# Attention and mixture of experts: the scatters of token assignments, one tile at a time

## The chip, the cores and the metric

The kernel runs on one NeuronCore of one Trainium2 chip. The metric is the device time of one execution in microseconds. Before the change it is 1081.88 us, the median of three runs (1081.15 to 1082.97).

A core has five engines, each with an instruction queue of its own that is worked off in order: TensorE (PE in the profile; its weight loads are PEld), VectorE (DVE), ScalarE (ACT), GpSimd (POOL) and SyncE (SP). Transfers are issued by SyncE, by ScalarE or, where rows are gathered or scattered by an index, by GpSimd.

## The reference

4096 tokens of 256 float32 values pass a causal attention and then a mixture of 8 experts, each with a layer norm ahead and the input added behind:

```python
x = x + attn(layernorm(x), Qw, Kw, Vw)      # softmax(Q K^T / sqrt(256) + causal mask) V
x = x + ffn(layernorm(x), ...)

def ffn(x):
    t = x @ W_in + b_in
    probs = softmax(t @ W_gate + b_gate)    # 8 experts
    topv, topi = top_k(probs, 2)            # each token goes to 2 experts
    topv = topv / sum(topv)
    for e in range(8):
        eout[e] = relu(t @ W1[e] + b1[e]) @ W2[e] + b2[e]      # 256 -> 1024 -> 256
    return sum_over_its_2_experts(topv * eout) @ W_out + b_out
```

So 8192 assignments of a token to an expert have to be sorted by expert, since the kernel computes only the two experts of each token.

## The kernel before

**Tiling.** A token block is 512 tokens (`TB`), that is 4 tiles of 128 (`TPB`), and there are 8 blocks (`NB`). A query tile is 256 tokens (`QB`), so there are 16 of them, numbered `g`, two to a block.

**Attention.** The loop at L1079 runs over `g`. Each turn records `scores(g + 1)` and then `attend(g)`. `scores` goes over chunks `c` of 256 keys up to the diagonal: 8 matmul records into one PSUM bank `ps` (tag `mm`, four buffers, L555), a copy to SBUF on ACT (`s`, L564), and from the second chunk on a running maximum on DVE (`mx`, L570). Between the `mx` of the first chunks stands `fill`: pieces of layer norm and transposes for later blocks, which `keep_in_program_order` pins one behind the other. `finish` (L594) transposes the maximum, subtracts it (DVE, L612) and exponentiates (ACT, L615). `attend` multiplies with the values (`po`, L633).

**Routing.** A block behind, `enter` (L353) makes `t` and the gate's logits of a block, writes `t` to the DRAM tensor `rows`, and `route` (L386) picks the two experts of each token, counts how many tokens each expert has had, and so finds each assignment's slot (`at`, L440). `slots` is a DRAM table with a stretch for each expert. `route` casts the four slot numbers of each of its two choices (`k`) to integers (`ati`, L441) and then issues, for each choice and tile, an indirect DMA from GpSimd that scatters 128 assignment numbers, 16 integers (`LINE`) each, to their slots (L443). That is 8 scatters to a block, 64 in all. They are declared free of dependence on one another, since slots are distinct.

The scatters of blocks 0 to 5 follow the attention of query tiles 3, 5, 6, 8, 10 and 12. Block 6 is routed in the middle of query tile 14 (`find`, L1112). Block 7, the last, is routed in the experts' loop at work item 1 (L1260).

**Other work on GpSimd.** Its queue also has the two steps of 1/sqrt(variance) of each layer norm (`ln_rstd`, L261 and L262), the addition of the output's bias to the residual (`x<-x,bout`, L1250), the gathers of expert rows (`h`, L824) and the scatters of results (`parts`, L997).

**Experts.** `plan` (L653) cuts each expert's slots into units. The work list has 17 units of kind a and 8 of kind b (256 slots, one expert), 8 of c (128 slots), 6 of d (twice 64 slots of two experts, two more only where needed) and one of z (256 late slots). Kind a is planned before query tile 14 from blocks 0 to 5, and its units read only slots of these. The loop at L1228 keeps three units ahead (`AHEAD`): `fetch_rows` loads a unit's slots (SyncE, L808) and gathers its rows (L824); `fetch_weights` loads four tiles of 512 KB for each expert and small biases (SyncE, L861 to L878) into buffers that an earlier unit frees; `turn_rows` transposes the rows on DVE (`hT`, L901); `hidden` does the first layer (`pm`, L921, activation on ACT at L930); `contribute` does the second (`pe`, L988), adds the bias on DVE (`y`, L996) and scatters (L997). At work item 3 the kernel takes the late unit: `take_late` (L752) loads 256 slots (`late_slot`, L762) and overwrites them in the table (`none`, L763). It has to wait for all scatters to `slots`, and what stands behind it in SyncE's queue, unit 7's slots and unit 6's weights first, waits with it. Here is the chain of these items in the code:

```python
take_late()                                        # L1231, at n == AHEAD
got[n + AHEAD + 1] = fetch_rows(work[n + AHEAD + 1])     # L1240
got[weighed] += fetch_weights(work[weighed], ...)        # L1243
```

**Order.** Within an engine the recording layer may move instructions that depend on nothing between them, but not those that `keep_in_program_order` pins. Tiles with a tag share its `bufs` buffers in turn, and the next user of a buffer waits for the last reader of the one before.

Of the kernel before, what the change touches and what calls it, by code (L numbers as in the profile page):

```python
# [37 lines left out]
def preln_attention_moe_kernel(  # L38
# [314 lines left out]
    def enter(b, zT, pool, behind=False):  # L353
# [29 lines left out]

        return lg

    def route(b, lg, seen, pool, behind=False):  # L386


        def small(name, w=1):
            return pool.tile([P, TPB, w], F32, tag=name, name=f"{name}{b}", bufs=2)  # L390

        def wide(a):
            return a.to_broadcast([P, TPB, NE])


        top = [small(f"top{k}") for k in range(TOPK)]
        hot = [small(f"hot{k}", NE) for k in range(TOPK)]
        prob, best = small("prob", NE), small("best")
        nc.vector.tensor_reduce(best, lg, AX.X, ALU.max)
        nc.vector.tensor_tensor(lg, lg, wide(best), ALU.subtract)  # L400
        nc.scalar.activation(prob, lg, AF.Exp)
        left = prob
        for k in range(TOPK):
            nc.vector.tensor_reduce(top[k], left, AX.X, ALU.max)
            nc.vector.tensor_tensor(hot[k], left, wide(top[k]), ALU.is_equal)
            nc.vector.tensor_tensor(hot[k], hot[k], rank, ALU.mult)
            nc.vector.tensor_reduce(best, hot[k], AX.X, ALU.max)
            nc.vector.tensor_tensor(hot[k], hot[k], wide(best), ALU.is_equal)
            if k == 0:
                left = small("left", NE)  # L410
                nc.vector.scalar_tensor_tensor(left, hot[0], -2.0, prob, ALU.mult, ALU.add)

        both = small("both", NE)
        nc.vector.tensor_tensor(both, hot[0], hot[1], ALU.add)
        past = small("past", NE)
        nc.vector.tensor_copy(past[:, 0, :], seen)
        for j in range(1, TPB):
            nc.vector.tensor_tensor(past[:, j, :], past[:, j - 1, :], both[:, j - 1, :], ALU.add)
        now = const.tile([P, NE], F32, tag=f"seen{b + 1}", name=f"seen{b + 1}")
        nc.vector.tensor_tensor(now, past[:, TPB - 1, :], both[:, TPB - 1, :], ALU.add)  # L420
        pk = ps_tr(f"pk{b}") if behind else ps_o(f"pk{b}")
        pkv = pk[:, : TPB * NE]
        done = nc.tensor.matmul(
            pkv, lhsT=before, rhs=both.rearrange("p t e -> p (t e)"), start=True, stop=False
        )
        if behind:
            tc.keep_in_program_order(done)
        nc.tensor.matmul(
            pkv, lhsT=ones, rhs=past.rearrange("p t e -> p (t e)"), start=False, stop=True
        )  # L430
        place = small("place", NE)
        nc.vector.tensor_tensor(
            place, pkv.rearrange("p (t e) -> p t e", e=NE), first, ALU.add
        )
        for k in range(TOPK):
            nc.vector.tensor_tensor(hot[k], hot[k], place, ALU.mult)
            at, ati = small(f"at{k}"), pool.tile(
                [P, TPB], I32, tag=f"ati{k}", name=f"ati{k}_{b}", bufs=2
            )
            nc.vector.tensor_reduce(at, hot[k], AX.X, ALU.add)  # L440
            nc.vector.tensor_copy(ati, at[:, :, 0])  # L441
            for j in range(TPB):
                put = nc.gpsimd.indirect_dma_start(  # L443
                    out=slots,
                    out_offset=bass.IndirectOffsetOnAxis(ap=ati[:, j : j + 1], axis=0),
                    in_=assign[:, TOPK * (b * TPB + j) + k :][:, :LINE],
                    in_offset=None,
                )

                tc.declare_no_dep(put.ins, group="slots", reason="slots are distinct")  # L450
                tc.add_to_no_dep_group("slots", put.ins)
                if b == NB - 1:
                    tc.add_to_no_dep_group("last", put.ins)
        tot = small("tot")
        nc.vector.tensor_tensor(tot, top[0], top[1], ALU.add)
        nc.vector.reciprocal(tot, tot)
        for k in range(TOPK):
            nc.vector.tensor_tensor(
                share[k][:, ts(b, TPB)], top[k][:, :, 0], tot[:, :, 0], ALU.mult
            )  # L460
        return now
# [77 lines left out]
    def scores(g, fill=()):  # L539
# [7 lines left out]
        for c in range(g + 1):  # L547
            ps = ps_mm(f"ps{g}_{c}")
            s = piece(f"s{g}_{c}", KU, QB)
            ss.append(s)  # L550
            for u in range(KU):
                kt = c * KU + u
                lo = u * P if c == g else 0
                for d in range(ND):
                    nc.tensor.matmul(  # L555
                        ps[:, u * QB + lo : (u + 1) * QB],
                        lhsT=zT[kt // TPB][:, kt % TPB, d, :],
                        rhs=qT[b][:, d, q * QB + lo : (q + 1) * QB],
                        start=(d == 0),
                        stop=(d == ND - 1),  # L560
                    )
            flat = s.rearrange("p u q -> p (u q)")
            if c < g:
                nc.scalar.copy(flat, ps)  # L564
                if c == 0:
                    mx = flat
                else:
                    old = mx
                    mx = attn.tile([P, TB], F32, tag="mx", name=f"mx{g}_{c}", bufs=2)
                    done = nc.vector.tensor_tensor(mx, ps, old, ALU.max)  # L570
                    for do in fill[len(fill) * (c - 1) // parts_of : len(fill) * c // parts_of]:
                        if done:
                            tc.keep_in_program_order(done)
                        done = do()
                    if fill and done:
                        tc.keep_in_program_order(done)
                continue
            for u in range(KU):
                on = slice(u * P, (u + 1) * P)
                nc.vector.tensor_tensor(  # L580
                    s[:, u, on], ps[:, u * QB + u * P : u * QB + (u + 1) * P], mask, ALU.add
                )
                if u + 1 < KU:
                    nc.scalar.copy(s[:, u, (u + 1) * P :], ps[:, u * QB + (u + 1) * P : (u + 1) * QB])
            if mx is None:
                nc.vector.tensor_copy(top, s[:, 0, :])
            else:
                nc.vector.tensor_tensor(top, mx[:, :QB], mx[:, QB:], ALU.max)
                nc.vector.tensor_tensor(top, top, s[:, 0, :], ALU.max)
            for u in range(1, KU):  # L590
                nc.vector.tensor_tensor(
                    top[:, u * P :], top[:, u * P :], s[:, u, u * P :], ALU.max
                )
# [310 lines left out]
    def hidden(item, got, hT, behind=()):  # L904
# [10 lines left out]
        for f in range(NF):  # L915
            if f % 2 == 0:
                mid.append(piece(f"mid_{k}{m}_{f}", 2, SB))
            pm = ps_mm(f"pm_{k}{m}_{f}")
            for c in range(ND):
                pin(  # L920
                    nc.tensor.matmul(  # L921
                        pm[:, :SB],
                        lhsT=w1[c][:, ts(f, P)],
                        rhs=hT[:, c, :],
                        start=(c == 0),
                        stop=(c == ND - 1),
                    )
                )
            pin(
                nc.scalar.activation(  # L930
                    mid[f // 2][:, f % 2, :], pm[:, :SB], AF.Relu, bias=c1[:, f : f + 1]
                )
            )
            if f > 2:
                for finish in behind[:2]:
                    finish()
                behind = behind[2:]
# [37 lines left out]
    def contribute(item, got, mid):  # L975
# [5 lines left out]
        for u in range(su):  # L981
# [3 lines left out]
            for f in range(NF):  # L985
                for j, (_, w2, _) in enumerate(sets):
# [7 lines left out]
                        )  # L994
                    )
            pin(nc.vector.tensor_tensor(y[:, u, :], pe[:, :D], c2, ALU.add))  # L996
            put = nc.gpsimd.indirect_dma_start(  # L997
                out=parts,
                out_offset=bass.IndirectOffsetOnAxis(ap=slot[:, u : u + 1], axis=0),
# [79 lines left out]
    for g in range(NT // KU):  # L1079
# [11 lines left out]
        fill = []  # L1091
        if q == 0 and b == NB - 1:

            early = seen
            tables["a"] = plan("a", early, NFULL, SB, 0)
            for n in range(AHEAD + 1):
                got[n] = fetch_rows(work[n])
# [8 lines left out]
        if q == 0 and b == NB - 1:  # L1106
# [5 lines left out]
            def find():  # L1112
                nonlocal seen
                seen = route(b - 1, lg, seen, attn, True)

            between[6], between[11] = [fetch_first], [find]
            weighed = AHEAD
# [110 lines left out]
    for n, item in enumerate(work):  # L1228
        steady = n >= AHEAD
        if n == AHEAD:  # L1230
            take_late()  # L1231
            quarters_left = nc.values_load(
                tables["d"][3][:1, :1],
# [96 lines left out]
```

## Time and profile before

| | |
|---|---|
| median of three runs | 1081.88 us (1081.15 to 1082.97) |
| the profiled execution's own time | 1071.75 us |
| its span, first instruction to last | 1070.0 us |
| instructions | 15770 |
| q0, the queue of GpSimd's DMAs | 8384 packets, 17.58 MB, 5.1% of the DMA engines' span |
| q1, SyncE's transfers | 139.67 MB, 42.4% |

The profile is of one execution. Busy times are per engine; a busy TensorE need not be at its peak, since matmuls overlap and their ends are modelled. A line of a group reads: source line, engine, operation, written tile <- read tiles, count, busy time, mean of one in ns, and the engine's idle time ahead of it with what ended it. A line of the timeline begins with the start in us and the duration. Roughly, the span holds the attention up to 564 us, the experts from there to 1031 us, and the output projection to the end.

### The profile page before, as it was taken

To read this page: it belongs to the slowest core of one execution; us is meant where nothing else is said; L and a number is where in the kernel's file an instruction comes from. 1 tells how busy PE (TensorE), PEld (TensorE's weight loads), DVE (VectorE), ACT (ScalarE), POOL (GpSimd) and SP (SyncE) were. 2 spreads that over 40 slices of the span, in tenths; PEclk is the share of its full clock that TensorE was granted. 3 is DMA by queue.
4 is the path that set the end of the run, shared out by engine and by line. 5 is a ranking of instruction groups with operands and counts; after the bars stand their busy time and mean duration, and the time that the engine had idled before them with its cause. 6 is when DMAs were issued, how large, how long until landed. Compare 5 with 4: busy or idle time off the path is not lost.

```text
span 1070.0 us, 15770 instructions
## 1 busy us (share of the span) xinstructions
PE 1062.3 (99%) x4973; PEld 882.9 (83%) x4973; DVE 674.6 (63%) x2114; ACT 332.4 (31%) x730; POOL 236.9 (22%) x289
## 2 busy tenths in 40 slices
PE   9999999999999999999999999999999999999998
PEld 6788888888888888888888887777778787777887
DVE  5877667564655546254665724858588786767636
ACT  2232233322432323242402221232323332323254
POOL 2104043103103000201222522232322322313110
PEclk9999999999999999999999999999999999999999
DMA  9422211121011011001655475887889896969285
GB/s 313 104 54 44 58 25 51 17 54 24 6 45 25 8 21 39 3 1 21 202 170 180 124 248 180 280 266 268 279 269 315 262 333 213 335 211 327 77 300 187
DMA packets 177995, 158.80 MB, mean 148 GB/s; under 512 B 82158, under 2 KB 157875, under 8 KB 177909
## 3 DMA queue, kind: packets, MB, share of 16 engines
q1 hardware_dynamic: 168980, 139.67, 42.4%
q0 software_dynamic: 8384, 17.58, 5.1%
q8 instruction: 40, 0.66, 0.3%
q10 hardware_dynamic: 544, 0.52, 0.1%
q14 instruction: 47, 0.38, 0.1%
HBM read 124.79 MB, written 26.38 MB: 141 GB/s over the span
## 4 chain that ended last, share of the span: by engine, by line
PE 97%; DVE 2%; POOL 0%; DMA 0%; issue 0%; SPq 0%; ACT 0%; DVEq 0%; POOLq 0%
PE po L633 21%; PE ps L555 21%; PE pm_a L921 11%; PE pe_a L988 11%; PE pe_b L988 5%; PE pm_b L921 5%; PE ph L362 3%; PE pm_c L951 3%; PE pf L1209 3%; PE pe_c L988 3%; PE pq L511 3%; PE pv L526 2%; PE pe_d L988 2%; PE pm_d L951 2%; PE pm_z L921 1%; PE pe_z L988 1%
## 5 line engine op out<-in xcount | busy, mean ns | idle before, releaser
L633 PE MATMUL po<-v,s 128*128 128x257 f32 x1056 | 237.9, 380 | 0.0
L555 PE MATMUL ps<-qT,zT 128*128 128x256 f32 x1088 | 233.3, 374 | 0.0
L555 PEld LDWEIGHTS ps<-qT,zT 128*128 128x128 f32 x1088 | 203.1, 190 | 28.0 <-issue 1.0
L633 PEld LDWEIGHTS po<-v,s 128*128 128x128 f32 x1056 | 197.2, 190 | 26.7
L564 ACT COPY s<-ps 128x512 f32<-128x512 f32 x120 | 70.2, 585 | 171.9 <-PE ps L555 132.6
L988 PE MATMUL pe_a<-w_a,mid_a 128*128 128x256 f32 x544 | 121.6, 380 | 0.0
L921 PE MATMUL pm_a<-hT_a,w_a 128*128 128x256 f32 x544 | 120.0, 379 | 0.0
L988 PEld LDWEIGHTS pe_a<-w_a,mid_a 128*128 128x128 f32 x544 | 102.6, 190 | 19.0 <-issue 5.6
L570 DVE TENSOR_TENSOR mx<-ps,mx 128x512 f32<-128x512 f32 x91 | 62.9, 691 | 83.7 <-ACT s L564 82.9
L930 ACT ACTIVATE mid_a<-pm_a,c_a 128x256 f32<-128x256 f32 x136 | 64.2, 472 | 165.1 <-PE pm_a L921 150.4
L921 PEld LDWEIGHTS pm_a<-hT_a,w_a 128*128 128x128 f32 x544 | 103.4, 190 | 14.1
L615 ACT ACTIVATE s<-s 128x512 f32<-128x512 f32 x120 | 72.2, 630 | 100.2 <-DVE s L612 100.2
L901 DVE STREAM_TRANSPOSE hT_a<-h_a 32x128 f32<-32x128 f32 x272 | 82.2, 302 | 3.8
L443 POOL DMA_INDIRECT slots<-assign,ati x64 | 62.5, 977 | 77.5 <-DVE ati L441 58.7
L612 DVE TENSOR_TENSOR s<-s,pmax 128x512 f32<-128x512 f32 x120 | 73.0, 679 | 7.3 <-PE pmax L608 7.3
L997 POOL DMA_INDIRECT parts<-y_a,slot_a x34 | 34.2, 1005 | 167.4 <-DVE y_a L996 138.0
L893 DVE STREAM_TRANSPOSE mid_c<-raw_c 32x256 f32<-32x256 f32 x128 | 55.8, 436 | 1.9
L988 PE MATMUL pe_b<-w_b,mid_b 128*128 128x256 f32 x256 | 56.8, 380 | 0.0
L921 PE MATMUL pm_b<-hT_b,w_b 128*128 128x256 f32 x256 | 56.6, 379 | 0.0
L988 PEld LDWEIGHTS pe_b<-w_b,mid_b 128*128 128x128 f32 x256 | 48.5, 190 | 9.4 <-issue 2.8
L921 PEld LDWEIGHTS pm_b<-hT_b,w_b 128*128 128x128 f32 x256 | 48.6, 190 | 6.6
L930 ACT ACTIVATE mid_b<-pm_b,c_b 128x256 f32<-128x256 f32 x64 | 30.1, 470 | 63.0 <-PE pm_b L921 63.0
(280 smaller groups left out, 1163.5 us busy)
## 6 DMA issues: line engine op xcount, KB each, us to landing
w_a<-in_L_ffn_W_dram SPq DMA_DIRECT2D x68, 512.0 KB, 6.0
w_d<-in_L_ffn_W_dram SPq DMA_DIRECT2D x48, 512.0 KB, 6.8
w_c<-in_L_ffn_W_dram SPq DMA_DIRECT2D x32, 512.0 KB, 8.1
w_b<-in_L_ffn_W_dram SPq DMA_DIRECT2D x32, 512.0 KB, 7.8
rows<-hr SPq DMA_DIRECT2D x16, 512.0 KB, 3.2
yp<-parts SPq DMA_DIRECT2D x14, 512.0 KB, 7.0
x<-in_L_attn_x_dram SPq DMA_DIRECT2D x7, 512.0 KB, 4.2
z1T<-z SPq DMA_DIRECT2D x112, 32.0 KB, 2.0
```

Of the source, the lines that this page charges most:

```text
L443: put = nc.gpsimd.indirect_dma_start(out=slots, out_offset=bass.IndirectOffsetOnAxis(ap=ati[:, j : j + 1], axis=0), in_=assign[:, TOPK * ( ...
L555: nc.tensor.matmul(ps[:, u * QB + lo : (u + 1) * QB], lhsT=zT[kt // TPB][:, kt % TPB, d, :], rhs=qT[b][:, d, q * QB + lo : (q + 1) * QB], ...
L564: nc.scalar.copy(flat, ps)
L570: done = nc.vector.tensor_tensor(mx, ps, old, ALU.max)
L612: nc.vector.tensor_tensor(s, s, pm[:, :QB].unsqueeze(1).to_broadcast([P, KU, QB]), ALU.subtract)
L615: nc.scalar.activation(s, s, AF.Exp)
L633: nc.tensor.matmul(po[u][:, : D + 1], lhsT=ss[c][:, k, ts(u, P)], rhs=vb[kt // TPB][:, kt % TPB, :], start=(kt == 0), stop=(kt == g * KU + u),
L893: pin(do())
L901: pin(do())
L921: nc.tensor.matmul(pm[:, :SB], lhsT=w1[c][:, ts(f, P)], rhs=hT[:, c, :], start=(c == 0), stop=(c == ND - 1),)
L930: nc.scalar.activation(mid[f // 2][:, f % 2, :], pm[:, :SB], AF.Relu, bias=c1[:, f : f + 1])
L988: nc.tensor.matmul(pe[ts(j, rest), :D], lhsT=mid[f][:, ts(u, P)][:, ts(j, rest)], rhs=w2[f // (NF // 2)][:, f % (NF // 2), :], start=(f == 0),
```

## The change

The scatters of a block are no longer issued by `route`. `route` puts eight small functions into a list, `puts`, and other places take one each: in `scores`, after every second `mx` (after every one while more than eight are waiting, and in the scores of query tile 14); in `hidden`, after every second activation, where the cast is made on ACT; in `contribute`, after each `y`. What block 6 puts on the list is taken at once in `find`. Each function casts one slot number per partition (128x1) into a buffer of its own tag `ati` with 8 buffers, and issues its scatter; the cast, not the scatter, is pinned in program order. The tile `at` now has four buffers for each choice instead of two. Two assertions say that the list is empty before `plan("a")` and before `take_late`.

```diff
+    puts = []
+
+    def put_tile(b, k, at, j, by=nc.vector.tensor_copy):
+
+        ati = attn.tile([P, 1], I32, tag="ati", name=f"ati{k}_{b}_{j}", bufs=8)
+        done = by(ati, at[:, j, :])
+        put = nc.gpsimd.indirect_dma_start(
+            out=slots,
+            out_offset=bass.IndirectOffsetOnAxis(ap=ati, axis=0),
+            in_=assign[:, TOPK * (b * TPB + j) + k :][:, :LINE],
+            in_offset=None,
+        )
+
+        tc.declare_no_dep(put.ins, group="slots", reason="slots are distinct")
+        tc.add_to_no_dep_group("slots", put.ins)
+        if b == NB - 1:
+            tc.add_to_no_dep_group("last", put.ins)
+        return done
+
+    def put_one(by=nc.vector.tensor_copy):
+
+        if puts:
+            tc.keep_in_program_order(puts.pop(0)(by=by))
+
     def route(b, lg, seen, pool, behind=False):
...
         for k in range(TOPK):
             nc.vector.tensor_tensor(hot[k], hot[k], place, ALU.mult)
-            at, ati = small(f"at{k}"), pool.tile(
-                [P, TPB], I32, tag=f"ati{k}", name=f"ati{k}_{b}", bufs=2
-            )
+            at = pool.tile([P, TPB, 1], F32, tag=f"at{k}", name=f"at{k}_{b}", bufs=4)
             nc.vector.tensor_reduce(at, hot[k], AX.X, ALU.add)
-            nc.vector.tensor_copy(ati, at[:, :, 0])
-            for j in range(TPB):
-                put = nc.gpsimd.indirect_dma_start(
-                    out=slots,
-                    out_offset=bass.IndirectOffsetOnAxis(ap=ati[:, j : j + 1], axis=0),
-                    in_=assign[:, TOPK * (b * TPB + j) + k :][:, :LINE],
-                    in_offset=None,
-                )
-
-                tc.declare_no_dep(put.ins, group="slots", reason="slots are distinct")
-                tc.add_to_no_dep_group("slots", put.ins)
-                if b == NB - 1:
-                    tc.add_to_no_dep_group("last", put.ins)
+            puts.extend(partial(put_tile, b, k, at, j) for j in range(TPB))
...
                     if fill and done:
                         tc.keep_in_program_order(done)
+
+                    if c % 2 or len(puts) > TOPK * TPB or g == NT // KU - 2:
+                        put_one()
                 continue
...
                     mid[f // 2][:, f % 2, :], pm[:, :SB], AF.Relu, bias=c1[:, f : f + 1]
                 )
             )
+            if f % 2:
+                put_one(nc.scalar.copy)
             if f > 2:
...
             pin(nc.vector.tensor_tensor(y[:, u, :], pe[:, :D], c2, ALU.add))
+            put_one()
             put = nc.gpsimd.indirect_dma_start(
...
+            assert not puts
             early = seen
             tables["a"] = plan("a", early, NFULL, SB, 0)
...
                 seen = route(b - 1, lg, seen, attn, True)
+                while puts:
+                    puts.pop(0)()
...
         if n == AHEAD:
+            assert not puts
             take_late()
```

## The prediction

> **What bounds the kernel now.** I read the page's busy times first, then TensorE's own waits, then the busy time by stretch, and only then the work that the change moves.
>
> ```profile
> PE 1062.3 (99%) x4973; PEld 882.9 (83%) x4973; DVE 674.6 (63%) x2114; ACT 332.4 (31%) x730; POOL 236.9 (22%) x289
> ...
> PEclk9999999999999999999999999999999999999999
> ```
>
> The share of the span is what to see: TensorE is idle for 1070.0 - 1062.3 = 7.7 us in all. GpSimd (POOL), which issues the moved scatters, is idle for four fifths of the span. The clock is full in all 40 slices. The waits of TensorE (engine, line, waited for: total, times, longest):
>
> ```profile
> PE warm L115 <- DVE zeros L112: 1.1, 1, 1.1
> PE pt L598 <- DVE top L589: 1.0, 1, 1.0
> ...
> PE pnc L667 <- DVE countb L669: 0.2, 1, 0.2
> ```
>
> The whole list has seven entries and none names a scatter to `slots`, GpSimd or the slot tables. The first two lie before the first routing. By stretch (length, then PE, PEld, DVE, ACT, POOL busy):
>
> ```profile
> 100.00:200.00 100.00, 99.88 (x462) 84.32 (x461) 64.53 (x204) 31.64 (x64) 21.81 (x23) 1.00 0.18 39
> 200.00:300.00 100.00, 100.00 (x467) 86.36 (x466) 58.80 (x159) 33.90 (x65) 16.32 (x16) 1.00 0.14 27
> ...
> 560.00:620.00 60.00, 59.83 (x285) 51.91 (x284) 36.97 (x192) 15.37 (x33) 21.46 (x21) 1.00 0.47 142
> ```
>
> These hold most of the eight bursts. TensorE misses 0.12 us in the first and 0.17 us in the last. The scatters themselves:
>
> ```profile
> L443 POOL DMA_INDIRECT slots<-assign,ati x64: 954/959/1231, 89.0 to 607.1; - x64
> ...
>   issue: 17.0, 56
> ...
> who waited for it (us, times):
> busy tenths in 40 slices 0002022002002000200020200000000000000000
> DMA to landing us min/median/max: 2.1/2.1/3.5
> ```
>
> One takes 0.96 us, and 17.0/56 = 0.30 us of issue lies ahead of each one that follows another: 1.27 us apiece, some 10 us for eight. Nobody's wait is put down to them here. SyncE's queue is not in that list, and it matters below.
>
> **What the skill says.** "Perfetto Trace Analysis", section Identifying the Most-Contended Engine, warns that matmul busy time is a poor measure of headroom and points to weight-load time. PEld is 83%, so 99% alone would not prove a bound. The chain of waits does: its share is PE 97%, in unbroken runs such as 80 matmul records of L555 in 17.01 us from 199.12, 0.21 us each. "DMA: Bandwidth & Descriptors", section Anatomy of one DMA, gives about 2.0 us plus bytes over bandwidth for a DMA from GpSimd; the 8 KB scatter lands in 2.1 us, which agrees. "VectorE: DVE Perf Modes", section on the TRN2 errata, says that small operations pay a fixed cost per instruction, so splitting one cast into four should cost four. The trace agrees: the 128x4 cast at L441 takes 167 ns, the 128x1 casts at L746 and L747 take 150 and 140 ns. "SBUF — State Buffer", section SBUF: two separate sides, warns that a DVE copy in a two-port mode can keep GpSimd from writing descriptors. The longest scatter of before is 1.23 us against a median of 0.96, so at most 0.3 us of this kind shows.
>
> **The change part by part.**
>
> *Removed*: 16 casts of 128x4 (16 x 0.167 = 2.7 us of DVE), and the standing of eight scatters together. *Added*: 60 casts of 128x1 on DVE (60 x 0.15 = 9.0 us) and 4 on ACT (nearest row: the 128x32 exp at L401, 0.23 us, so 0.9 us). DVE goes from 674.6 to about 681 us, ACT to about 333; both stay far under the span. The 64 scatters stay, with the same bytes. Comparing the built programs, the order of instructions on TensorE and on SyncE is unchanged; DVE, ACT and GpSimd orders change only around these casts and scatters.
>
> *Blocks 0 to 5, in the scores.* A chunk of 256 keys is 8 matmul records, 1.73 us. A cast now follows every second `mx` (every one where more than eight wait, and in the scores of query tile 14). DVE in the scores of tile 9:
>
> ```profile
> 210.29 0.69 DVE L570 TENSOR_TENSOR mx<-ps,mx 128x512 f32<-128x512 f32 x1 [0.42 <-ACT s L564]
> 212.02 0.69 DVE L570 TENSOR_TENSOR mx<-ps,mx 128x512 f32<-128x512 f32 x1 [1.03 <-ACT s L564]
> ```
>
> A chunk without fill leaves DVE 1.03 us idle, and a 0.15 us cast fits. With fill the idle time falls to about zero (around 208.6 us). There the cast may delay `mx`, but the PSUM tag `mm` has four buffers: chunk c of tile 9 starts at 199.12 + 1.73 c, so the bank of chunk 4, whose `mx` ends at 209.26, is next written at chunk 8, 212.96, 3.7 us later. A cast takes 0.15 of that. Cost on TensorE: 0. If that cover went, each chunk would cost the cast, at most 60 x 0.15 = 9 us. GpSimd needs 1.27 us per scatter against 1.73 us per chunk, so it keeps up; `x<-x,bout` (L1250, 2.36 us, waiting up to 5.6 us for `z`) stands between scatters and can put it about four back. A cast waits only for the scatter eight earlier. Behind GpSimd's scatters stand the two `rstd` steps: they wait at most for one or two scatters instead of up to eight, and their reader (`z`, L271) is fill that TensorE does not wait for. Slots are read first at 506 us, after `plan("a")`; the last scatter of block 5 now goes with key chunk 8 of tile 14, near 446 us. Cost and gain: 0.
>
> *Block 6.* `find` empties the list at once: eight casts of 0.15 where two took 0.40 us with their wait, so DVE is about 0.8 us later at 538 us. TensorE has 27 us of `po` in front of it there, and DVE is idle for 8.8 us before 563 (both from the timeline). Cost 0.
>
> *Block 7, in the experts.* Two scatters go with contribution 1 (DVE), four with hidden layer 3 (ACT), two with contribution 2 (DVE). Each 0.23 us cast on ACT stands behind a 0.47 us activation in a pair pitch of 1.73 us; 0.94 + 0.23 fits. Two effects remain. First, in DVE's new order five instead of four 0.30 us transposes of `hT` stand ahead of `countb`, less the two casts that leave: about +0.2 us, straight onto the wait of `pnc` above. Second, SyncE is in order, and its load of `late_slot` waits for all scatters:
>
> ```profile
> 607.11 0.96 POOL L443 DMA_INDIRECT slots<-assign,ati  x1 [0.30 <-issue]
> ...
> 610.46 0.56 SPq L762 DMA_DIRECT2D late_slot<-slots  x1
> 612.73 0.68 SPq L763 DMA_DIRECT2D slots<-none  x1
> 615.14 1.56 SPq L808 DMA_DIRECT2D slot_d<-slots  x2
> 617.21 1.86 SPq L861 DMA_DIRECT2D w_a<-in_L_ffn_W_dram  x2
> ```
>
> The new last scatter follows the second `y_a` of contribution 2, which DVE starts at 619.21: cast done near 619.9, `parts` on GpSimd to 621, scatter from 621.2 to 622.2, landed at 624.3. `late_slot` is then loaded at 624.5, 14 us late, and so is all behind it on SyncE: `slots<-none`, two `slot_d`, the first weights of work item 6, its second weights, the slot loads of items 8 and 9, both experts of item 7. Who waits? Item 6's hidden layer:
>
> ```profile
> 646.64 7.07 PE L921 MATMUL pm_a<-hT_a,w_a 128*128 128x256 f32 x32
> ```
>
> Its weights would be issued at 631.2 and, with the page's median of 6.0 us, land at 637.2: 9.4 us in hand (23.4 before). Item 7's four 512 KB first-layer tiles are needed at 660.6; items 6 and 7 together want 4 MB by then from 631, 29 us at some 300 GB/s being 8.7 MB. The gather `h_d` moves from 620 to about 633, its transposes start at 647.2; scatters of `parts` 3 queue behind it for 4 us and have 20. By 659 the loads are again held by the buffers alone. Cost 0.
>
> *Sum.* 1071.75 us, the profiled execution's own time (span 1070.0 plus 1.75 around it), + 0.2 = 1071.95. The median of the runs shown is 10.13 us above that execution. Nothing here changes what lies outside the span, so I carry it over: 1081.88 + 0.2 = 1082.1. The unknowns: the `pnc` wait 0 to +0.5; the casts in the scores 0 to +9 (I take 0, for the 3.7 us of bank slack); SyncE's lateness 0 to about +4 (0, for the 9.4 us); the end of the bursts -1 to 0, since all waits of TensorE between 100 and 620 us are under 1 us together.
>
> **Rivals.**
>
> *Faster, 1079.5, chance 0.10.* The bursts cost something in the executions that were not profiled, which are 10.13 us longer. If each of the eight cost TensorE the 0.3 us by which the matmuls of `pk` for one block stood late at 170.9 us, this is 8 x 0.3 = 2.4 us. For it: 10 us during which GpSimd's in-order queue serves nothing else. Against it: TensorE is 100.00 us busy between 200 and 300, bursts included.
>
> *Slower, 1085.7, chance 0.08.* The late last block. If the last scatter lands more than 9.4 us later than I have it (GpSimd held by `parts`, or the ACT casts waiting in order), or the weights need more than 15.4 us instead of 6.0 because delayed loads crowd, item 6 starts late. At 27 us of total lateness instead of 14 it is 27 - 23.4 = 3.6 us on TensorE. For it: SyncE loses 14 us of issue time in the hungriest stage. Against it: weights have over 9 us left.
>
> *Slower, 1085.1, chance 0.03.* A cast waits for its `ati` buffer while GpSimd is behind, and holds `mx` past the 3.7 us, say twice by 1.5 us: 3 us. It needs GpSimd eight scatters behind; it is about four at worst.
>
> *The change does nothing to the bursts of blocks 0 to 5* is excluded: the new order has them apart. That block 6 stays a burst is in the forecast.
>
> **How the numbers follow.** No measurable change, 1082.1, has chance 0.79; its own range is 1081.0 to 1083.3 (the spread of the runs before, about 0.9 each way, and the 0 to 0.5). A measurement of this kernel can tell about 0.2%, 2.2 us, from no change. The range over all is 1079.8 to 1084.8, leaving out the far ends of the rivals. Faster 0.10, same 0.79, slower 0.11.
>
> **What would show it.** Right: TensorE busy still near 1062 with about 8 us idle; DVE about 681; scatters at their 0.96 us but spread; `late_slot` loaded near 624 and item 6's hidden layer still starting within 0.5 us of 646.8; the `pnc` wait at 0.3 to 0.5. Wrong: a wait of TensorE for weights near 647 or 661, for `mx` in the scores, or a shorter TensorE total.

## The result, and the profile after

The changed kernel takes 1072.11 us (median of 4 runs, 1071.80 to 1074.04), the kernel before 1081.84 us beside it (4 runs, 1081.15 to 1082.97). The ratio is 0.9913, with a 95% interval of 0.9896 to 0.993. The change takes away 9.7 us; the prediction had 1082.1 us, no change.

The profiled executions tell nothing of this. That of the kernel before had a span of 1070.0 us and a time of 1071.75 us; that of the changed kernel has 1070.0 and 1071.80. So the two profiles are equally long, as predicted, and it is in the timed runs that the kernel before was slower. The profiler is not the reason for that: the third batch below has profiled executions of 1081 us. The page of the changed kernel, busy times and granted clock:

```profile
PE 1062.0 (99%) x4973; PEld 882.8 (83%) x4973; DVE 675.2 (63%) x2158; ACT 332.4 (31%) x734; POOL 237.8 (22%) x289
...
PEclk9999999999999999999999999999999999999999
```

TensorE's waits in it (total, times, longest):

```profile
PE pbias L191 <- DMA brows<-in_L_ffn_b_dram: 1.1, 1, 1.1
...
PE pnb L681 <- DVE restz L763: 0.3, 1, 0.3
PE pnc L681 <- DVE countb L683: 0.2, 1, 0.2
```

The wait of `pnb` is new, 0.3 us, and that of `pnc` has stayed at 0.2. Nothing names the scatters. SyncE's queue behind the last scatter (start and length in us):

```profile
625.41 0.56 SPq L776 DMA_DIRECT2D late_slot<-slots  x1
...
632.56 0.90 SPq L875 DMA_DIRECT2D w_a<-in_L_ffn_W_dram  x2
```

TensorE's hidden layer of work item 6, which needs these weights:

```profile
646.79 7.07 PE L935 MATMUL pm_a<-hT_a,w_a 128*128 128x256 f32 x32
```

`late_slot` is loaded 15 us later than before and the hidden layer still starts where it did. What has to be explained is therefore not in these two traces. It needs an execution of the kernel before that takes 1081 us, with a profile.

### The profile page after: what moved, and what is told of

It reads as the page before. It is cut to its first block, busy times and chain, and to the rows that moved or that the text cites. A ratio compares the mean times of both kernels' runs of the same rounds, so it can differ in the third digit from the quotient of the medians.

```text
span 1070.0 us, 15840 instructions
## 1 busy us (share of the span) xinstructions
PE 1062.0 (99%) x4973; PEld 882.8 (83%) x4973; DVE 675.2 (63%) x2158; ACT 332.4 (31%) x734; POOL 237.8 (22%) x289
```

## The experiments

The experiments ran in four batches, each on one chip, with the kernel before timed on the same chip. That turned out to matter: on the first chip the kernel before took 1071.55 us (39 runs, 1071.31 to 1072.01), on the other three 1081.43, 1081.70 and 1081.38.

### First batch: bursts against spread scatters

Three versions of the changed kernel. The first empties the list at once in every block:

```diff
             puts.extend(partial(put_tile, b, k, at, j) for j in range(TPB))
+            while puts:
+                puts.pop(0)()
```

The second does so only in the last block (`while puts and b == NB - 1`), the third in all but the last (`while puts and b < NB - 1`). The kernel before, unchanged, ran with them.

> The kernel before, unchanged, so that an execution of about 1081 us can be read. The profile on record is of one execution of 1071.75 us, ten under the median of the others, 1081.84. Theory A (eight scatters in a row cost time in most executions): this profile is of an execution near 1081 us with a span near 1080, and about 10 us of TensorE waits more than the 7.7 us idle on record, at one place or at a few; the place tells which block. Theory B (the ten microseconds lie outside what the kernel does, in the chip used): this run is near 1072 like the changed kernel, ratio 1.00. If the profile shows 1071 again while the timed runs show 1081, the place has to be found by the times of the variants.

> The changed kernel, with each block's eight scatters taken from the list at once in the routing, so eight in a row again, but with eight 128x1 casts and the new tiles. Theory A1 (it is the scatters' standing together): as before, about 1081 us. Theory C (it is the separate casts, buffers or tiles, not the spacing): as the changed kernel, about 1072 us.

> The changed kernel, with block 7 alone issued eight in a row (blocks 0 to 5 spread, block 6 in a row as in both). Theory A2 (the loss lies in the attention, blocks 0 to 5): 1072 us, as changed. Theory A3 (the loss lies in the experts, where block 7's burst stands): 1081 us.

> The changed kernel, with blocks 0 to 5 issued eight in a row and block 7 alone spread. Theory A2 (loss in the attention): 1081 us. Theory A3 (loss in the experts): 1072 us. If every burst costs a share, about 1079 us here and 1074 with block 7 alone in a row.

Measured: 1071.49, 1071.67, 1071.72 and 1071.88 us, ratios 1.0000 (0.9991 to 1.0009), 1.0001 (0.9992 to 1.0010), 1.0002 (0.9993 to 1.0011) and 1.0003 (0.9994 to 1.0012). On this chip it makes no difference how the scatters stand: the kernel before is as short as the changed one. Here it is as the prediction said: nothing waits for a burst. That cannot be all, since the change did gain 9.7 us elsewhere.

### Second batch: is the gain real, and are the prediction's margins?

The changed kernel again; then with three idle maxima on VectorE behind each cast in the scores; then with the last scatter of block 7 held back by a chain of 20, or 80, small GpSimd operations.

```diff
-                        put_one()
+                        if puts:
+                            put_one()
+                            for _ in range(3):
+                                tc.keep_in_program_order(
+                                    nc.vector.tensor_tensor(mx, mx, mx, ALU.max)
+                                )
```

```diff
+            if len(puts) == 1 and k == "a" and m == 2:
+                last, nil = puts[0].args[2], const.tile([P, 1], F32, tag="nil", name="nil")
+                nc.gpsimd.tensor_tensor(nil, y[:, u, :1], zeros[:, :1], ALU.mult)
+                for _ in range(80):
+                    nc.gpsimd.tensor_tensor(nil, nil, ones[:, :1], ALU.mult)
+                nc.gpsimd.tensor_tensor(last[:, 3, :], last[:, 3, :], nil, ALU.add)
+                puts.pop(0)(by=nc.gpsimd.tensor_copy)
```

> The changed kernel, unchanged, timed in turn with the kernel before on one chip. Theory B (the change itself moves nothing; the 1081.84 us belong to the place or time at which the kernel before was measured): ratio 1.000 within 0.001, by the profiles +0.2 to +0.4 us (1071.55 to about 1071.9), since TensorE waits 0.3 us for pnb in the changed kernel and not in the one before. Theory A (the change is worth nine microseconds): ratio 0.991. If this chip gives the kernel before near 1081, theory B has both kernels near 1081.

> The changed kernel with three more maxima of 128x512 (0.69 us each, 2.07 together) behind each of the casts in the scores (mx with itself, so no value changes). If the bank slack of 3.7 us carries the casts, 0.15 us each are free and 2.07 us are not: where every chunk has one, DVE needs 2.76 us of a chunk of 1.73 and the slack is gone after some four chunks. Estimate, (2.76 - 1.73) times the consecutive chunks, plus 3 us of fill where there is any, less 3.7: 2 us at tile 7, 6 at tile 8, 4 at tile 10, 4 at tile 14: about 16 us more, 1088 us, with waits of TensorE in the scores for mx. A rival in which DVE is not near the path at all: 1072 us.

> The changed kernel with the last scatter of block 7 held back by a chain of 20 small GpSimd operations (some 0.2 us each, as the 128x4 operation of L261: 0.23). late_slot is then loaded about 5 us later than the 625.4 us of the changed kernel, item 6's first weights are issued near 637.5 and land near 643.5, before 646.8. If the slack of the late chain is some 8 us: no loss, 1072 us. If the chain is already on the path: 1077 us.

> The same with a chain of 80 operations, so some 19 us later: item 6's first weights are issued near 651.5 and land near 657.5 for a hidden layer due at 646.8. Slack of 8 us: 19 - 8 = 11 us more, about 1083 us, and TensorE waits for w_a near 647. If the chain had far more room than I think: 1072 us.

*Changed kernel again*: 1072.44 us, ratio 0.9920 (0.9906 to 0.9933). The gain is real on this chip.

*Heavy casts*: 1088.55 us, ratio 1.0068 (1.0051 to 1.0084). TensorE's waits:

```profile
PE ps L566 <- DVE mx L581: 5.6, 8, 1.8
PE pv L537 <- issue: 3.4, 1, 3.4
```

About 2 us more per cast (3 x 0.69) does reach TensorE, through the PSUM banks that `mx` releases. A bare cast does not: the first of these lines is missing in the changed kernel. The cover that the prediction named is there, and it is not endless. That the total came out at the 1088 us expected is in part luck: of 16 us more, 5.6 are waits for `mx`; the wait of `pv`, 3.4 us, has no releaser in the profile, and not all of the rest is traced.

*Late by 5*: 1071.93 us, ratio 0.9915 (0.9900 to 0.9930); `late_slot` is loaded at 631.61 us, 6.2 us after the changed kernel's, and nothing is lost. *Late by 19*: 1087.01 us, ratio 1.0051 (1.0036 to 1.0067). In the second, `late_slot` is loaded at 647.77 us, 22.4 us after the changed kernel's, and item 6's hidden layer (start, length, idle time before it) is late:

```profile
658.34 10.33 PE L935 MATMUL pm_a<-hT_a,w_a 128*128 128x256 f32 x32 [11.23 <-DMA w_a<-in_L_ffn_W_dram]
```

So SyncE's chain has 22.4 - 11.2 = 11.2 us in hand in the changed kernel (the prediction worked out 9.4). The same line shows a second thing: the layer takes 10.33 instead of 7.07 us. By stretch (length, then PE, PEld, DVE, ACT, POOL busy, granted clock, DMA share, GB/s):

```profile
650.70:664.35 13.65, 5.94 (x13) 4.36 (x14) 2.10 (x9) 0.97 (x3) 2.00 (x2) 0.50 0.62 186
664.35:668.60 4.25, 4.25 (x21) 3.71 (x21) 1.68 (x8) 2.35 (x5) 0.99 (x1) 1.00 1.01 389
```

The clock is down after the stall. The Trainium skill, "TensorE: Matmul & The Clock Gate", Part 1, describes it: after an idle window of about 3.4 us the array runs at half rate until it has been busy for a window. This trace agrees: the clock falls to 0.50 at 650.7 us, 3.6 us into the stall of 11.2 us, and comes back at 664.35, 6.0 us after it; the layer takes 3.3 us more. And it gives the clue to the 10 us: the kernel before showed a mean clock of 0.995 to 0.998 in its runs on this chip, the changed kernel 1.000. A clock below 1 is a sign that TensorE *stalls* in those executions, long enough to lose its clock.

### Third batch: the stall itself

The kernel before with a profile, and the three versions of the first batch, this time on a chip where the kernel before takes 1081.70 us (32 runs).

> The kernel before, unchanged, for a profile of it on a chip where it takes about 1081 us. Theory A (TensorE really stalls there, behind one of the eight-scatter bursts): span about 1080, granted clock below 1.0, and one TensorE wait of 3 to 8 us in the list of waits, at a place where GpSimd's eight scatters stand. Theory B (the extra time has nothing to do with the scatters): the wait is elsewhere, or spread over the whole span. If this chip gives about 1071.5 us, as one chip did, the run tells nothing on this.

> The changed kernel with every block's eight scatters emptied in route, as before. Where the kernel before takes about 1081 us: Theory A, the bursts cost the 10 us, says this also takes about 1081 (ratio 1.00). Theory B says it takes about 1072 (ratio 0.992), since the rest of the changed kernel is kept. Where before takes about 1071.5, both say 1071.5.

> The changed kernel with only the last block's eight scatters in a row; the other blocks spread. Theory A with the stall in the last block: about 1081 (ratio 1.00). Theory A with the stall in one of the blocks 0 to 5: about 1072 (ratio 0.992). Where before takes about 1071.5, both say 1071.5.

> The changed kernel with blocks 0 to 6 in a row and only the last block spread. Theory A with the stall in the last block: about 1072 (ratio 0.992). Theory A with the stall in blocks 0 to 5: about 1081 (ratio 1.00). Where before takes about 1071.5, both say 1071.5.

| version | us | ratio to before | TensorE stalls in its profile |
|---|---|---|---|
| before | 1081.48 | 0.9996 (0.9988 to 1.0005) | `pmax` 3.4, `pm_a` 3.0 |
| all blocks at once | 1081.48 | 0.9998 (0.9991 to 1.0005) | `pmax` 3.5, `pm_a` 3.0 |
| last block at once | 1076.65 | 0.9951 (0.9934 to 0.9967) | `pm_a` 3.1 |
| blocks 0 to 6 at once | 1077.64 | 0.9959 (0.9945 to 0.9973) | `pmax` 3.6 |

Theory A is right, with two stalls instead of one; each half of the change removes one of them. The changed kernel with its bursts put back is as long as the kernel before, so nothing else in the change matters by more than about 1 us. (Block 6 is a burst in every version of the changed kernel; no stall stands near it.) The first lines of TensorE's waits in the kernel before, span 1080.0 us:

```profile
PE pmax L608 <- DVE m L603: 3.4, 1, 3.4
PE pm_a L921 <- ACT mid_a L930: 3.0, 1, 3.0
```

Neither line is in the list of the profiled execution that the prediction was made from. And the stretches around the two stalls, in this execution:

```profile
97.00:101.40 4.40, 1.00 (x6) 0.54 (x4) 0.42 (x1) 0.00 (x0) 1.68 (x2) 1.00 0.22 31
102.80:106.20 3.40, 3.40 (x8) 2.27 (x7) 2.82 (x8) 3.38 (x7) 0.00 (x0) 0.50 0.00 0
614.00:617.00 3.00, 0.04 (x1) 0.00 (x0) 1.16 (x11) 0.51 (x2) 0.61 (x1) 1.00 0.21 57
618.20:621.60 3.40, 3.40 (x9) 2.70 (x8) 3.17 (x23) 1.10 (x3) 0.36 (x1) 0.50 0.48 155
```

In the second and fourth line TensorE is busy all the time, but at a clock of 0.50: 8 and 9 matmuls where a stretch of this length has 15 or more in the profiled execution of before. Half clock for 3.4 us loses 1.7 us. The sum is 3.4 + 3.0 + 2 x 1.7 = 9.8 us, against 1080.0 - 1070.0 = 10.0 us of span.

Here the measurement differs from the 3.4 us of idleness that the page gives: stalls of 3.0 and 3.4 us were followed by half clock. How much of it follows varies. In the profile of the version with blocks 0 to 6 at once the clock is 0.50 for 6.83 us (100.05 to 106.88) instead of 3.41. And the 32 runs of the kernel before on this chip fall into three groups: 1079.7 to 1080.3 us at a mean clock of 0.998, 1081.1 to 1081.9 at 0.997, 1082.6 to 1083.0 at 0.995. The steps fit one, two and three stretches of 3.41 us at half clock, an estimate from these numbers.

Why does TensorE stall? First stall: VectorE's row maximum of the transposed `top`. In the profiled execution of the kernel before (start, length, idle time ahead):

```profile
97.25 0.42 DVE L603 TENSOR_REDUCE m<-pt 128x2 f32<-128x256 f32 x1 [3.86 <-PE pt L598]
```

The same instruction in this execution:

```profile
100.92 0.42 DVE L603 TENSOR_REDUCE m<-pt 128x2 f32<-128x256 f32 x1 [7.62 <-remote]
```

The transposes it reads are done at the same point in both, near 97.1 us. It runs 3.7 us later, with nothing else on VectorE in between; "remote" is only the profile's word for a releaser that it has no record of. GpSimd in the same execution:

```profile
98.02 0.96 POOL L443 DMA_INDIRECT slots<-assign,ati  x1 [0.30 <-issue]
```

This is the last of block 0's eight scatters. `m` runs 1.9 us after it has ended. The second stall lies at block 7's burst (603.39 to 613.30 us). VectorE in this execution:

```profile
611.31 0.31 DVE L901 STREAM_TRANSPOSE hT_a<-h_a 32x128 f32<-32x128 f32 x1 [1.65 <-issue]
...
613.69 0.16 DVE L706 CAST base_ib<-baseb 128x8 int32<-128x8 f32 x1
614.92 0.17 DVE L682 TENSOR_SCALAR nowc<-nowc 128x8 f32<-128x8 f32 x1 [1.07 <-DVE base_ib L706]
```

ScalarE, whose four steps TensorE waits for:

```profile
616.50 1.57 ACT L930 ACTIVATE mid_a<-pm_a,c_a 128x256 f32<-128x256 f32 x4 [14.27 <-remote]
```

SyncE's queue, where two transfers of 0.38 us each take this long from the first to the end of the second:

```profile
609.19 6.84 SPq L872 DMA_DIRECT2D w_a<-in_L_ffn_W_dram  x2
```

In the first profiled execution the same two transfers take 2.11 us, and the same steps of VectorE follow each other almost without a rest. To measure it I set the instruction starts of this execution against those of the first profiled one, counted from each burst's first scatter. In blocks 1 to 5 VectorE falls 1.5 to 4.1 us behind, in blocks 0 and 7 3.7 and 5.1 us, and in block 6 SyncE 2.7 us. It begins some 6 to 10 us after the burst's first scatter, where that can be seen, and is over some 2 to 4 us after the last, where the engine has slack to catch up. TensorE is late in two places only, where the late step is the very next thing that it needs.

The traces also tell on which kind of chip a profile was taken. SyncE sets a register ahead of a transfer (`MOVE`); here are those of one weight load in the kernel before as first profiled, the kernel before in this batch, and the changed kernel as first profiled (count, then shortest, median and longest in ns):

```profile
L872 SPq MOVE w_a<-in_L_ffn_W_dram x34: 29/29/29, 512.5 to 831.9; - x34
L872 SPq MOVE w_a<-in_L_ffn_W_dram x34: 4/29/700, 517.8 to 842.1; - x34
L886 SPq MOVE w_a<-in_L_ffn_W_dram x34: 16/29/542, 512.4 to 832.3; - x34
```

Of all 327 such steps none takes 0.1 us or more in the first batch's four profiles and in the first profile of the kernel before. In each of the other profiles 16 to 30 do, by up to 0.8 us, and all but one of these lie within half a microsecond of a GpSimd transfer, many of them far from any row of scatters (a third of all such steps lie so). So the first profile of the kernel before bears the mark of the first batch's chip, and that of the changed kernel the mark of the other three: the two profiles compared above were most likely taken on chips of different kinds.

### Fourth batch: what in the burst does it

Again on a chip where the kernel before takes 1081 us (1081.38, 7 runs). Four in a row and then one at a time; only the middle blocks in a row; the changed kernel with eight additional scatters in a row in each block's `route` (third cut below, where `P` is 128); and the same with 16 of the 128 rows.

```diff
+            while k == 0 and puts:
+                puts.pop(0)()
```

```diff
+            while puts and 0 < b < NB - 1:
+                puts.pop(0)()
```

```diff
+            ia = pool.tile([P, TPB], I32, tag=f"ia{k}", name=f"ia{k}_{b}", bufs=2)
+            nc.vector.tensor_copy(ia, at[:, :, 0])
+            for j in range(TPB):
+                extra = nc.gpsimd.indirect_dma_start(
+                    out=dump,
+                    out_offset=bass.IndirectOffsetOnAxis(ap=ia[:P, j : j + 1], axis=0),
+                    in_=assign[:P, TOPK * (b * TPB + j) + k :][:, :LINE],
+                    in_offset=None,
+                )
```

> The changed kernel, but of each block the first choice's four scatters go in a row in route, and only the second choice's four one at a time. On a chip where the kernel before takes about 1081 us, the other engines fall behind only from 5.8 to 8.8 us after a burst's first scatter, that is from the fifth to the seventh. Theory 'a backlog that builds up over more than four': no stall, about 1072 us (ratio 0.992). Theory 'every scatter in a row costs its share': half the loss of each stall, about 1075 to 1077 us. Where before takes about 1071.5, both say 1071.5.

> The changed kernel with blocks 1 to 6 in a row and only blocks 0 and 7 spread. If the 10 us are two stalls, 3.4 us at the maxima of block 0's attention and 3.0 us at the hidden layer under block 7's scatters, each with 1.7 us of half clock behind it, and the other six bursts are covered by TensorE's work in hand: about 1072 us (ratio 0.992), though VectorE still falls 1.5 to 4 us behind in those six. If every burst costs its part: six eighths of the loss stay, about 1079.5. Where before takes about 1071.5, both say 1071.5.

> The changed kernel as it is, with the real scatters spread, and besides in route eight extra scatters in a row of the same rows and places into a second table that nobody reads. It adds work and leaves none out. Theory 'eight scatters in a row slow the other engines, whatever they carry': the stalls are back, 1081 us or some us more (ratio 1.00 or above). Theory 'it is the real scatters' place in the dependences' (someone waits for them): about 1072. Where before takes about 1071.5, both say 1071.5 to 1072.

> As the run with extra scatters, but each extra scatter carries the first 16 of its 128 rows. Theory 'the rows (descriptors) make the backlog': no stall, about 1072 us (ratio 0.992). Theory 'the number of scatter instructions makes it': stalls as with the full extra scatters, 1081 us or more. Where before takes about 1071.5, both say 1071.5 to 1072.

*Four at once*: 1072.18 us, ratio 0.9917 (0.9900 to 0.9933). No gain is lost. In block 0 two of the scores' scatters follow the four directly, so that six stand in a row there, up to 96.43 us; `m` then runs at 98.06 us, some 0.8 us late:

```profile
98.06 0.42 DVE L619 TENSOR_REDUCE m<-pt 128x2 f32<-128x256 f32 x1 [4.78 <-PE pt L614]
```

*Middle at once*: 1072.35 us, ratio 0.9917 (0.9900 to 0.9934). Six of the eight bursts are free (the sixth, block 6, stands in the changed kernel too). VectorE is held in them all the same; here in block 1, whose last scatter ends at 149.34 us, an instruction that otherwise takes 0.41 us:

```profile
148.98 3.03 DVE L605 TENSOR_TENSOR top<-top,s 128x256 f32<-128x256 f32 x1
152.05 0.29 DVE L607 TENSOR_TENSOR top<-top,s 128x128 f32<-128x128 f32 x1
```

*Extra scatters*: 1116.09 us, ratio 1.0332 (1.0310 to 1.0354). *Small extra scatters*: 1122.42 us, ratio 1.0386 (1.0362 to 1.0410). Nobody reads the second table, so it isn't a dependence on the real scatters. The real ones now follow the extra ones without a gap (ten in a row in block 0), and the stalls are longer and more than I had expected: five new lines of waits, 26 us together, with a mean clock of 0.983. One kind is new. TensorE itself stands idle while the profile names nothing that it waits for, in the first and in the second of these runs:

```profile
PE po L659 <- issue: 8.8, 9, 1.6
PE po L659 <- issue: 13.3, 12, 1.7
```

With 16 rows instead of 128 it is no better. These scatters are a little shorter (`ap=ia[:16, ...]` and `assign[:16, ...]`), so they stand closer. Their line, with the shortest, median and longest in ns:

```profile
L468 POOL DMA_INDIRECT dump<-assign,ia x64: 842/846/1105, 88.8 to 648.9; - x64
```

Block 0's `m` in the same execution, whose data are ready near 97 us as before:

```profile
103.45 0.42 DVE L629 TENSOR_REDUCE m<-pt 128x2 f32<-128x256 f32 x1 [10.28 <-remote]
```

So it goes with how many scatters follow each other, and not with their rows or bytes. The number of packets is not told apart from it: the profile counts 32 for a scatter of 16 rows as for one of 128 (10432 in GpSimd's queue in both runs). Against 97.25 us in the first profile, block 0's `m` is 0, 0.8, 3.7, 4.7 and 6.2 us late with two scatters that stay apart from the rest, six, eight, ten and ten short ones in a row. A control stands in the second batch: there GpSimd worked through 80 small arithmetic operations, from 621.8 to 644.6 us, and VectorE's and ScalarE's instructions in that time stood within 0.1 us of those of the changed kernel on the same chip. GpSimd being busy is not the cause; its scatters one behind the other are.

## Why the prediction was wrong, step by step

- **TensorE's order and waits in the profiled execution**: right. 1062.0 us busy, 8.0 idle (said: near 1062 and about 8). The time of the profiled execution was to be 1071.95 and is 1071.80. The 0.2 us was put on `pnc`; `pnb` got 0.3.
- **Casts in the scores at nothing, for the banks' slack**: right, and shown by the heavy casts. VectorE was to be busy for 681 us and is for 675.2: one cast has 0.14 us, but it starts before the instruction ahead of it has ended (one at 210.73 us, behind an `mx` that runs from 210.12 to 210.81), so the net is 0.6 us instead of 6.4.
- **The late last block at nothing**: right. `late_slot` at 625.41 us (said 624.5), item 6's first weights at 632.56 (said 631.2), and about 11 us in hand (said 9.4). That rival is excluded at the real lateness.
- **"The median of the runs shown is 10.13 us above that execution. Nothing here changes what lies outside the span, so I carry it over"**: this is the step that failed. In the sum it is also the term for the end of the bursts, -1 to 0, which measured about -10. The 10.13 us do not lie outside the span. An execution of 1081.81 us has a span of 1080.0; what lies around the span is 1.8 us in it as in the short ones. The 10 us are two stalls and the half clock behind each, made by the very bursts that the change takes apart. The view had the sign of it: three runs within 1.8 us of each other, and the profiled execution 9.4 us below the lowest of them. That is no spread, it is an execution of another kind, most likely of another chip, and the profile was read as if it stood for all. That the prediction was right about its own profile follows from this and does not bear on the timed runs.
- **The rival "faster"** named the right place, the bursts in the executions that were not profiled, and mis-sized it: 0.3 us for each of eight, 2.4 us, where it is 5 us for each of two and nothing for six. It was bounded by the waits of an execution in which the effect is absent. The stretches shown begin at 100 us and leave out block 0's burst, 89 to 99 us, where the first stall proved to be; the stretch held against the rival, 200 to 300, has one burst. With "the bursts cost what the executions differ by" its bound would have been the 10.13 us themselves.
- **GpSimd's queue as the only thing that a burst holds up**: the prediction looked for those who wait *for* GpSimd. It is the other engines, which wait for nothing of it, that a burst holds up.

Shown: the two places, their sizes, that either half of the change removes its own stall, that six bursts are free, and that the number of scatters in a row counts and not their rows. Not shown: by what way a row of scatters holds VectorE, ScalarE and SyncE. The trace has an instruction that runs for 3.03 us instead of 0.41, others that start late, and a pair of transfers that takes SyncE 6.84 us to issue, so that it is not one engine's matter; behind rows of eight TensorE's own matmuls go on meanwhile, behind longer ones they too pause, for no wait that the profile names. The Trainium skill's page that the prediction cites, "SBUF — State Buffer", section SBUF: two separate sides, describes a lock between VectorE and GpSimd that goes to whichever starts first. It could hold VectorE, but no run tests it, and it would leave ScalarE and SyncE alone, which were up to 5 us late here. Nor is it known why one chip of the four doesn't do it.

## What to carry to other kernels

If the timed runs agree with each other and the profiled execution lies apart from them, first ask what those runs do that the profile doesn't show, whether it comes from the same chip, and look at their spans and granted clocks; the difference is not overhead until the span says so. Where the next step of VectorE or ScalarE is one that TensorE needs at once, don't put many GpSimd scatters directly behind each other: four to six cost nothing here, eight cost 5 us; one every few microseconds costs nothing. And count a TensorE stall of 3 us or more with the half clock that can follow it, 1.7 us or more.

## What the hardware showed that was not expected

- The same program took 1071.5 us on one chip and 1081.4 to 1081.7 us on three others, each steady (at most 4 us between the lowest and the highest run).
- On those three chips, from six GpSimd scatters in a row on, at 1.15 to 1.27 us apiece, the other engines fall behind, by up to 5 us for eight; 80 GpSimd arithmetic operations in a row do nothing of the kind. On the first chip rows of eight do nothing either (block 0's `m` at 97.08 us in the kernel before).
- On the three chips a register step of SyncE near a GpSimd transfer took up to 0.8 us instead of 0.03, also away from the rows; on the first chip none did.
- TensorE stalls of 3.0 to 3.6 us were followed by 3.4 to 6.8 us at a clock of 0.50 in the profiles; one of 11.2 us by 6.0 us of it, which cost 3.3 us.
